# Edge weights scaled, and part of the window sums copied out of PSUM, by VectorE in place of ScalarE

## The chip, the cores and the metric

The kernel runs on one core of one Trainium2 chip. The metric is the device time of one launch in microseconds (us); lower is better. A core has several engines that run their own instruction streams in order and wait for one another through semaphores: TensorE (PE in the profile, with its weight loads as PEld), VectorE (DVE), ScalarE (ACT), GpSimd (POOL) and SyncE (SP). ScalarE, GpSimd and SyncE issue DMAs here. Matmuls write to PSUM, a small memory that GpSimd and the DMAs cannot use; everything else on the chip lies in SBUF.

## The reference

A graph layer on 12,500 nodes and 400,000 edges. For each edge, a small network turns 16 edge numbers into 192 weights; the source node's mapped row (160 numbers) is multiplied by them and by the edge's own four numbers, and the products are summed over the edges of each destination node. The edges come sorted by destination.

```python
h = maximum(layernorm(x), 0)                # per node
x0, x1 = h[:, :64], h[:, 64:].reshape(n, 32, 3)
y0 = x0 @ W_l1_0 * a / sqrt(64);  y1 = einsum('nuc,uv->nvc', x1, W_l1_1) * a / sqrt(32)
w = silu(edge16 @ fc_W1 / sqrt(16)) @ fc_W2 / sqrt(64)        # 192 weights per edge
w_a, w_b, w_c, w_d = w[:, :64], w[:, 64:128], w[:, 128:160], w[:, 160:]
e0, e1 = e4[:, :1], e4[:, 1:]               # e4: four numbers per edge
mid_a = w_a * y0[src] * e0
mid_d = w_d * einsum('euc,ec->eu', y1[src], e1) / sqrt(3)
mid_b = (w_b * y0[src])[:, :, None] * e1[:, None, :]
mid_c = (w_c * e0)[:, :, None] * y1[src]
z = sum over edges, by dst, of mid_a, mid_d (96 numbers) and mid_b, mid_c (96 x 3)
out = x + c_s * self_connection(h) + c_x * linear(z) * a
```

The scalar e0 multiplies only w_a and w_c. The kernel keeps the weights in the order a, c, b, d, so that these are the first 96 of the 192 columns.

## The kernel before, in words

**Nodes first.** A first stage normalizes the nodes, maps them, and writes the mapped rows to a table y_d in device memory. Its lines 324 to 384 (batch_norm, transposes, L373's copies out of PSUM, L384's addition) matter here only as rows from which durations can be read. L129 to L181 then prepare the edges' offsets.

**The edge loop.** The edges stand in 3125 tiles of 128. A batch b is four tiles (GT = 4), so there are 782 batches. Three tiles that follow each other share a window of 32 nodes (WT = 3, WN = 32), four windows make a group (GW = 4), so a group is 12 tiles or three batches, k = 0, 1, 2. A batch goes through these steps:

- `load(b)` (L456 to L476): GpSimd issues four indirect DMAs (gathers, L474), one for each tile, that fetch the source nodes' rows from y_d into a tile yg. There are 12 buffers of yg, and loads are issued ten batches ahead (AHEAD = 10). Ten batches, numbers 12, 24 and so on to 120, take their rows from a second table yr_d by one DMA of SP instead (L471). SP also loads the edge network's input, xe (L465).
- `hidden_pair` (L483, L488): every fourth batch, TensorE computes the hidden layer for two pairs of batches and ScalarE applies the activation (hT).
- `weigh(b)` (L505): four matmuls put the 192 weights of each edge into a PSUM tile pw, of which there are two. Then `scale` lets ScalarE multiply the first 96 columns of each tile by e0 in place (L421, four instructions of 128x96) and copy e1 and the edge's window offset behind the weights (L422, 16 numbers).
- `select(b)` (L536, L538): VectorE builds the selection matrix sel from pw's last columns: which of the 32 nodes an edge belongs to, alone and times each of e1's three numbers.
- `products(b)` (L427 to L434): VectorE multiplies yg with the weights in pw, into pr. L427 is the first instruction to read yg, so it waits for the gathers.
- `sums(b)` (L556): TensorE multiplies sel with pr for each tile and sums a window in a PSUM tile pz, of which there are two. When a window is complete, ScalarE copies it to the SBUF tile zs: 192 columns from the last 32 partitions (L561), and 64 columns from each of three other sets of 32 partitions (L563).
- `turn`, `linear`, `add` (L571 to L594), for the group before, in batches k = 0, 1, 2: TensorE transposes zs, ScalarE copies it out (za, L573), TensorE applies the output weights, ScalarE copies that out (os, L582, L583) while VectorE makes a placement matrix (place, L586), and TensorE places the rows among 256 nodes.
- `accumulate` (L599 to L603), in batch k = 2: VectorE loads the node tile's number into a register and adds the result to acc, two instructions.

TensorE, ScalarE and VectorE run these in the order in which the program writes them (a manual schedule); the semaphores are put in by the framework. GpSimd and SP run their loads in order, as buffers allow. The order of one batch is this:

```python
            for b in range(NB):
                ...
                if b + 2 < NB:
                    weigh(b + 2)
                if g:
                    (turn, linear, add)[k](g - 1)
                if b + 1 < NB:
                    select(b + 1)
                    products(b + 1)
                if g and k == K - 1:
                    accumulate(g - 1)
                    leave_before(g)
                sums(b)
                if b % 4 == 0 and b + 4 < NB:
                    hidden_pair((b + 4) // 2)
```

After the loop the last group is finished and the rest of acc is stored. A second path (L659 on), for edges too far from their window, is in the program, but these inputs do not enter its loop; it also calls `scale`.

Of the kernel before, what the change touches and what calls it, by code (L numbers as in the profile page):

```python
# [12 lines left out]
AF = mybir.ActivationFunctionType  # L13
# [5 lines left out]
P = 128  # L19
# [5 lines left out]
NW = 2 * M0 + 2 * M1  # L25
# [20 lines left out]
def kernel(  # L46
# [19 lines left out]
    nc = tc.nc  # L66
# [7 lines left out]
    NB = (T + GT - 1) // GT  # L74
# [342 lines left out]

    def scale(pw, ev, n):

        for k in range(n):  # L420
            nc.scalar.activation(pw[:, k, 0:96], pw[:, k, 0:96], AF.Copy, scale=ev[:, k, 0:1])  # L421
        nc.scalar.activation(pw[:, :n, NW:NW + 4], ev[:, :n, 1:5], AF.Copy)  # L422

    def multiply(pr, tmp, wt, yg, n):

        y1 = yg[:, :n, M0:].rearrange("p t (c u) -> p t c u", c=3)
        nc.vector.tensor_tensor(tmp[:, :n, 0:3, :], y1, wt[:, :n, NW:NW + 3].unsqueeze(3).to_broadcast([P, n, 3, M1]),  # L427
                                ALU.mult)
        nc.vector.tensor_reduce(tmp[:, :n, 3, :], tmp[:, :n, 0:3, :].rearrange("p t c u -> p t u c"), AX.X, ALU.add)  # L429
        nc.vector.tensor_mul(pr[:, :n, 192:PC], wt[:, :n, 96:160], yg[:, :n, 0:M0])  # L430
        nc.vector.tensor_mul(pr[:, :n, 0:M0], wt[:, :n, 0:M0], yg[:, :n, 0:M0])  # L431
        nc.vector.tensor_mul(pr[:, :n, 96:192].rearrange("p t (c u) -> p t c u", c=3),  # L432
                             wt[:, :n, M0:96].unsqueeze(2).to_broadcast([P, n, 3, M1]), y1)
        nc.vector.tensor_mul(pr[:, :n, M0:96], wt[:, :n, 160:NW], tmp[:, :n, 3, :])  # L434

    with (
# [11 lines left out]
        blocks, ev4, hids, rows, wts, sels, z_ps, z_sb, zT, o_sb, prs, sums_ps = ({} for _ in range(12))  # L448

        def tiles_of(b):  # L450
            return list(range(b * GT, min((b + 1) * GT, T)))
# [4 lines left out]
        def load(b):  # L456
            blk = b * GT // BT
            if blk not in blocks:

                xe = ld.tile([P, 512], F32, name="xe")  # L460
                v = e16[blk * P:(blk + 1) * P, :].rearrange("(s k f) (h c) -> s h f k c", s=4, k=2, h=2)
                for s in range(4):
                    for h in range(2):
                        lo = 32 * s + FC_IN * h
                        nc.sync.dma_start(xe[lo:lo + FC_IN, :].rearrange("p (k c) -> p k c", k=2), v[s, h])  # L465
                blocks[blk] = xe
            yg = ygp.tile([P, GT, D], F32, name="yg")
            rows[b] = yg
            r = made(b)
            if r is not None:  # L470
                nc.sync.dma_start(yg, by_tile(yr_d[r * GT * P:(r + 1) * GT * P, :]))  # L471
                return
            for k, t in enumerate(tiles_of(b)):
                nc.gpsimd.indirect_dma_start(  # L474
                    out=yg[:, k, :], out_offset=None, in_=y_d,
                    in_offset=bass.IndirectOffsetOnAxis(ap=src_sb[:, t:t + 1], axis=0))  # L476
# [14 lines left out]
        def hidden_pair(s):  # L491

            pair = [i for i in (s, s + 1) if 2 * i < NB]
            for i, ph in [(i, hidden(i)) for i in pair]:
                activate(i, ph)

        def weigh(b):
            hT = hids[b // 2]
            pw = p_w.tile([P, GT, 256], F32, name="pw")
            n = len(tiles_of(b))  # L500
            for k in (0, 2, 1, 3):
                if k < n:
                    r = slice(FC_H * (k // 2), FC_H * (k // 2 + 1))
                    o = P * (b % 2 * 2 + k % 2)
                    nc.tensor.matmul(pw[:, k, 0:NW], hT[r, o:o + P], w2[r, :], start=True, stop=True)  # L505
            scale(pw, e4_of(b), n)
            wts[b] = pw

        def e4_load(q):

            if q * EG < NG and q not in ev4:
                lo, hi = q * EG * TG, min((q + 1) * EG * TG, TP)
                raw = ld.tile([P, EG * TG, 4], F32, name="raw")
                nc.sync.dma_start(raw[:, :hi - lo, :].rearrange("p t c -> p (t c)"), e4[:, lo * 4:hi * 4])
                ev = evp.tile([P, EG * TG, 5], F32, name="ev")
                ev4[q] = ev, raw, lo, hi - lo

        def e4_join(q):
            if q in ev4:
                ev, raw, lo, n = ev4[q]  # L520
                nc.scalar.activation(ev[:, :n, 0:4], raw[:, :n, :], AF.Copy)
                nc.scalar.activation(ev[:, :n, 4:5], drel[:, lo:lo + n].unsqueeze(2), AF.Copy)

        def e4_of(b):
            g, k = divmod(b, TG // GT)
            o = g % EG * TG + k * GT
            return ev4[g // EG][0][:, o:o + GT, :]
# [13 lines left out]
        def products(b):  # L541
            wt, yg = wts.pop(b), rows.pop(b)
            pr = prod.tile([P, GT, PC], F32, name="pr")
            tmp = prod.tile([P, GT, 4, M1], F32, name="tmp")
            multiply(pr, tmp, wt, yg, len(tiles_of(b)))
            prs[b] = pr

        def sums(b):
            pr = prs.pop(b)
            for k, t in enumerate(tiles_of(b)):  # L550
                g, w = t // TG, t // WT % GW
                if t % WT == 0:
                    z_ps[g, w] = p_z.tile([P, 512], F32, name="pz")
                pz = z_ps[g, w]
                last = t % WT == WT - 1 or t == T - 1
                nc.tensor.matmul(pz[:, 0:PC], sels[g][:, t % TG, :, :], pr[:, k, :], start=t % WT == 0, stop=last)  # L556
                if last:
                    if w == 0:
                        z_sb[g] = post.tile([P, ZC], F32, name="zs")
                    pz, zs = z_ps.pop((g, w)), z_sb[g][WN * w:WN * (w + 1), :]  # L560
                    nc.scalar.activation(zs[:, 0:192], pz[96:P, 0:192], AF.Copy)  # L561
                    for c in range(3):
                        nc.scalar.activation(zs[:, 192 + M0 * c:192 + M0 * (c + 1)],  # L563
                                             pz[WN * c:WN * (c + 1), 192:PC], AF.Copy)
# [41 lines left out]
        def leave_before(g):  # L606

            for k, (lo, i) in enumerate(FLOORS):
                if lo == g:
                    store(FLOORS[k - 1][1] if k else 0, i)  # L610
# [5 lines left out]
        with order:  # L616
            for b in range(min(AHEAD, NB)):
                load(b)
            e4_load(0)
            e4_join(0)  # L620
            hidden_pair(0)
            weigh(0)
            if NB > 1:
                weigh(1)
            select(0)
            products(0)
            for b in range(NB):
                g, k = divmod(b, K)
                if b + AHEAD < NB:
                    load(b + AHEAD)  # L630
                q, r = divmod(b, EG * K)
                if r == 0:
                    e4_load(q + 1)
                if r == EG * K - 4:
                    e4_join(q + 1)
# [4 lines that stand above are left out]
                if b + 1 < NB:  # L640
                    select(b + 1)
                    products(b + 1)
                if g and k == K - 1:
                    accumulate(g - 1)
                    leave_before(g)
# [3 lines that stand above are left out]
            for h in ([NG - 2] if NG > 1 else []) + [NG - 1]:  # L649
                for k, stage in enumerate((turn, linear, add, accumulate)):  # L650
                    if h == NG - 1 or min(k, K - 1) > (NB - 1) % K:
                        stage(h)
                        if k == 3:
                            leave_before(h + 1)
# [4 lines left out]
    with (  # L659
# [10 lines left out]
        n = nc.values_load(far_i[0:1, 0:1], min_val=0, max_val=1)  # L670
        with tc.For_i(0, n, 1) as _:
            with tc.For_i(0, ZR, P) as r:
                nc.sync.dma_start(z_d[ds(r, P), :], zero)
            with tc.For_i(0, TP // GT, 1) as g:
# [4 lines left out]
                ev = fp.tile([P, GT, 5], F32, name="f_ev")  # L679
# [19 lines left out]
                pw = fpw.tile([P, GT, 256], F32, name="f_pw")  # L699
# [7 lines left out]
                for k in range(GT):  # L707
# [6 lines left out]
                    for c in range(3):  # L714
                        nc.scalar.activation(m[:, 192 + M0 * c:192 + M0 * (c + 1)], pr[:, k, 192:PC], AF.Copy,
                                             scale=ev[:, k, 1 + c:2 + c])
# [10 lines left out]
                    pz = fpp.tile([P, ZC], F32, name="f_pz")  # L727
                    nc.tensor.matmul(pz, sel, m, start=True, stop=True)
                    zs = fp.tile([P, ZC], F32, name="f_zs")
# [63 lines left out]
```

## Time and profile before

| what | value |
|---|---|
| median of three runs | 4068.4 us (4061.18 to 4073.2) |
| the profiled execution | 4061.72 us |
| its span | 4059.8 us |
| TensorE's mean granted clock | 0.933 |
| busy: PE, DVE, ACT, POOL | 3235.3, 2922.8, 2692.2, 3018.0 us |
| gathers (L474) | 3085, mean 948 ns |
| edge loop, first L427 to last | 208.0 to 4044.1 us |

The profile is of one execution on the chip. The span is what the profiler recorded; the execution's own time is 1.9 us longer. Times are in microseconds from the start of the span unless marked ns. A row of the costliest groups names line, engine, operation, the tiles (output<-inputs), the shapes (partitions x elements) and the count; then busy time and the mean of one in ns; then the engine's idle time just before these instructions and what ended most of it. "issue" means that the engine waited for nothing that the profile shows. In the waits, a line gives engine, instruction, what it waited for, the total, the number of times and the longest. DVEq is VectorE's sequencer, which handles waits and registers ahead of the engine itself.

### The profile page before, as it was taken

Reading aid. Unit: us, or ns where it says so; the run is one execution under the profiler, and the core shown is the slowest. Engines: PE = TensorE matmul, PEld = TensorE weight load, DVE = VectorE, ACT = ScalarE, POOL = GpSimd, SP = SyncE. Lnnn points to the kernel's source line nnn. Section 1 sums busy time; section 2 is a strip of 40 time slices with the busy share of each in tenths; the row PEclk is TensorE's granted clock in tenths of the full one; section 3 lists DMA queues with packets and bytes.
Section 4 is the critical chain, followed back from the end, with each engine's and each line's share of the span. In section 5 each row is a group of like instructions: output and inputs, shape, how many; then the busy total and the mean of one; then the engine's idle time right before and its main releaser. Section 6 shows DMA issues by size and latency. Waiting matters only on the chain.

```text
span 4059.8 us, 62554 instructions
## 1 busy us (share of the span) xinstructions
PE 3235.3 (80%) x17505; PEld 2347.5 (58%) x17505; DVE 2922.8 (72%) x7558; ACT 2692.2 (66%) x9543; POOL 3018.0 (74%) x3177
## 2 busy tenths in 40 slices
PE   6588888878787787887877887878777788778777
PEld 5466666555555555555555555555555555555555
DVE  7787777776777777777777777767777777777776
ACT  5477777766666666666666666666666666666665
POOL 7477777777777777777777777777777777777776
PEclk9899999999989989999999999999999989999998
DMA  6333333332322233323233332323232323243233
GB/s 192 88 84 83 80 83 80 76 76 74 77 74 74 74 76 74 77 74 76 72 76 75 75 76 74 74 74 77 74 76 74 76 72 76 75 124 75 72 81 78
DMA packets 244949, 326.49 MB, mean 80 GB/s; under 512 B 67290, under 2 KB 194342, under 8 KB 244342
## 3 DMA queue, kind: packets, MB, share of 16 engines
q0 software_dynamic: 151280, 256.22, 25.7%
q1 hardware_dynamic: 74322, 54.52, 4.7%
q10 hardware_dynamic: 18996, 11.72, 0.9%
q8 instruction: 141, 2.31, 0.2%
q14 instruction: 210, 1.72, 0.1%
HBM read 302.92 MB, written 19.28 MB: 79 GB/s over the span
## 4 chain that ended last, share of the span: by engine, by line
DVE 25%; POOL 23%; DMA 21%; issue 21%; PE 5%; ACT 1%; DVEq 1%; ACTq 0%; POOLq 0%
POOL yg L474 23%; DMA yg<-y_d,src_sb 21%; DVE tmp L429 5%; DVE tmp L427 5%; DVE pr L432 3%; DVE pr L431 2%; DVE acc L603 2%; DVE pr L434 2%; DVE sel L538 2%; PE pz L556 2%; DVE pr L430 2%; DVE sel L536 1%; PE pw L505 1%; PE px L483 1%; DVE place L586 1%
## 5 line engine op out<-in xcount | busy, mean ns | idle before, releaser
L474 POOL DMA_INDIRECT yg<-y_d,src_sb x3085 | 2925.3, 948 | 982.5 <-issue 745.8
L556 PE MATMUL pz<-pr,sel 128*128 128x256 f32 x6250 | 1623.9, 407 | 0.3 <-DVE pr L434 0.3
L421 ACT ACTIVATE pw<-pw,ev 128x96 f32<-128x96 f32 x3125 | 985.3, 315 | 858.3 <-PE pw L505 769.6
L556 PEld LDWEIGHTS pz<-pr,sel 128*128 128x128 f32 x6250 | 1237.4, 208 | 157.6 <-issue 0.9
L505 PE MATMUL pw<-w,hT 64*128 64x192 f32 x6250 | 758.5, 363 | 667.1 <-DVE pr L434 657.5
L427 DVE TENSOR_TENSOR tmp<-yg,pw 128x384 f32<-128x384 f32 x782 | 432.8, 553 | 972.3 <-DMA yg<-y_d,src_sb 970.8
L505 PEld LDWEIGHTS pw<-w,hT 64*128 64x128 f32 x6250 | 514.6, 194 | 1060.9 <-DVE pr L434 893.9
L563 ACT ACTIVATE zs<-pz 32x64 f32<-32x64 f32 x3126 | 669.9, 214 | 41.8
L429 DVE TENSOR_REDUCE tmp<-tmp 128x128 f32<-128x384 f32 x782 | 463.7, 593 | 27.0
L538 DVE TENSOR_TENSOR sel<-sel,pw 128x384 f32<-128x384 f32 x782 | 432.7, 553 | 27.0
L561 ACT ACTIVATE zs<-pz 32x192 f32<-32x192 f32 x1042 | 337.8, 324 | 148.3 <-PE pz L556 125.7
L432 DVE TENSOR_TENSOR pr<-pw,yg 128x384 f32<-128x384 f32 x782 | 428.8, 548 | 0.0
L483 PE MATMUL px<-xe,w 32*128 32x512 f32 x782 | 301.0, 656 | 81.8 <-issue 72.7
L488 ACT ACTIVATE hT<-px 128x512 f32<-128x512 f32 x391 | 218.5, 595 | 179.8 <-PE px L483 172.9
L431 DVE TENSOR_TENSOR pr<-pw,yg 128x256 f32<-128x256 f32 x782 | 324.1, 414 | 0.0
L430 DVE TENSOR_TENSOR pr<-pw,yg 128x256 f32<-128x256 f32 x782 | 323.8, 414 | 0.0
L536 DVE TENSOR_TENSOR sel<-iota,pw 128x128 f32<-128x128 f32 x782 | 218.8, 280 | 58.0 <-ACT pw L422 57.6
L580 PE MATMUL px<-wc,za 128*128 128x96 f32 (+1 forms) x1566 | 257.3, 305 | 0.4 <-ACT za L573 0.4
L580 PEld LDWEIGHTS px<-wc,za 128*128 128x128 f32 x1566 | 211.6, 205 | 62.2 <-issue 45.2
L434 DVE TENSOR_TENSOR pr<-pw,tmp 128x128 f32<-128x128 f32 x782 | 220.4, 282 | 0.0
L594 PE MATMUL px<-os,place 128*128 128x160 f32 x1044 | 219.0, 334 | 0.5 <-ACT os L583 0.5
L603 DVE SCALAR_TENSOR_TENSOR acc<-px,a_sb,acc 128x160 f32 x522 | 198.5, 380 | 12.2 <-PE px L594 2.7
(97 smaller groups left out, 1742.0 us busy)
## 6 DMA issues: line engine op xcount, KB each, us to landing
yg<-y_d,src_sb POOLq DMA_INDIRECT x3085
xe<-in_e SPq DMA_DIRECT2D x784, 32.0 KB
y_d<-ys ACTq DMA_DIRECT2D x12, 640.0 KB
acc<-in_x SPq DMA_DIRECT2D x11, 640.0 KB
out<-acc SPq DMA_DIRECT2D x11, 640.0 KB
raw<-in_e SPq DMA_DIRECT2D x32, 192.0 KB
yr_d<-ys ACTq DMA_DIRECT2D x5, 640.0 KB
yg<-yr_d SPq DMA_DIRECT2D x10, 320.0 KB
```

The costliest lines, as they stand in the source:

```text
L421: nc.scalar.activation(pw[:, k, 0:96], pw[:, k, 0:96], AF.Copy, scale=ev[:, k, 0:1])
L427: nc.vector.tensor_tensor(tmp[:, :n, 0:3, :], y1, wt[:, :n, NW:NW + 3].unsqueeze(3).to_broadcast([P, n, 3, M1]), ALU.mult)
L429: nc.vector.tensor_reduce(tmp[:, :n, 3, :], tmp[:, :n, 0:3, :].rearrange("p t c u -> p t u c"), AX.X, ALU.add)
L430: nc.vector.tensor_mul(pr[:, :n, 192:PC], wt[:, :n, 96:160], yg[:, :n, 0:M0])
L431: nc.vector.tensor_mul(pr[:, :n, 0:M0], wt[:, :n, 0:M0], yg[:, :n, 0:M0])
L432: nc.vector.tensor_mul(pr[:, :n, 96:192].rearrange("p t (c u) -> p t c u", c=3), wt[:, :n, M0:96].unsqueeze(2).to_broadcast([P, n, 3, M1]) ...
L474: nc.gpsimd.indirect_dma_start(out=yg[:, k, :], out_offset=None, in_=y_d, in_offset=bass.IndirectOffsetOnAxis(ap=src_sb[:, t:t + 1], axis=0))
L505: nc.tensor.matmul(pw[:, k, 0:NW], hT[r, o:o + P], w2[r, :], start=True, stop=True)
L538: nc.vector.tensor_tensor(sel[:, :, 0:3, :], sel[:, :, 3:4, :].to_broadcast([P, n, 3, WN]), wt[:, :n, NW:NW + 3].unsqueeze(3).to_broadcast ...
L556: nc.tensor.matmul(pz[:, 0:PC], sels[g][:, t % TG, :, :], pr[:, k, :], start=t % WT == 0, stop=last)
L563: nc.scalar.activation(zs[:, 192 + M0 * c:192 + M0 * (c + 1)], pz[WN * c:WN * (c + 1), 192:PC], AF.Copy)
L580: nc.tensor.matmul(po[:m, lo:hi], za[:, k, :m], wc[:, k, lo:hi], start=k == 0, stop=k == 1)
```

## The change

VectorE does three things that ScalarE did. `scale` becomes two VectorE instructions on a whole batch: a copy of e4's columns, and one multiplication of 128 x 4 x 96 elements in place in PSUM, with e0 stretched over 96 columns. The call of `scale` is taken out of `weigh` and put into a new function `apply`, which stands after `products(b + 1)` for batch b + 2, so on VectorE the scaling of a batch comes one batch ahead of its use. And the first 192 columns of each window are copied out of PSUM by VectorE. The three copies of 64 columns, the activations, za and os stay on ScalarE. In the built program, ScalarE's three copies of a window wait for VectorE's copy of the same window. The number of gathers, matmuls and DMAs is the same.

```diff
     def scale(pw, ev, n):
 
-        for k in range(n):
-            nc.scalar.activation(pw[:, k, 0:96], pw[:, k, 0:96], AF.Copy, scale=ev[:, k, 0:1])
-        nc.scalar.activation(pw[:, :n, NW:NW + 4], ev[:, :n, 1:5], AF.Copy)
+        nc.vector.tensor_copy(pw[:, :n, NW:NW + 4], ev[:, :n, 1:5])
+        nc.vector.tensor_mul(pw[:, :n, 0:96], pw[:, :n, 0:96], ev[:, :n, 0:1].to_broadcast([P, n, 96]))
...
-            scale(pw, e4_of(b), n)
             wts[b] = pw
+
+        def apply(b):
+
+            scale(wts[b], e4_of(b), len(tiles_of(b)))
...
-                    nc.scalar.activation(zs[:, 0:192], pz[96:P, 0:192], AF.Copy)
+                    nc.vector.tensor_copy(zs[:, 0:192], pz[96:P, 0:192])
...
             weigh(0)
+            apply(0)
             if NB > 1:
                 weigh(1)
             select(0)
             products(0)
+            if NB > 1:
+                apply(1)
             for b in range(NB):
...
                 if b + 1 < NB:
                     select(b + 1)
                     products(b + 1)
+                if b + 2 < NB:
+                    apply(b + 2)
                 if g and k == K - 1:
                     accumulate(g - 1)
                     leave_before(g)
```

## The prediction

> **What bounds the kernel now.** I read the page's shares of the span first, then its costliest groups, then two long windows of the edge loop, then the waits, then the order of time.
>
> ```profile
> PE 3235.3 (80%) x17505; PEld 2347.5 (58%) x17505; DVE 2922.8 (72%) x7558; ACT 2692.2 (66%) x9543; POOL 3018.0 (74%) x3177
> ...
> L474 POOL DMA_INDIRECT yg<-y_d,src_sb x3085 | 2925.3, 948 | 982.5 <-issue 745.8
> ...
> L421 ACT ACTIVATE pw<-pw,ev 128x96 f32<-128x96 f32 x3125 | 985.3, 315 | 858.3 <-PE pw L505 769.6
> ...
> L427 DVE TENSOR_TENSOR tmp<-yg,pw 128x384 f32<-128x384 f32 x782 | 432.8, 553 | 972.3 <-DMA yg<-y_d,src_sb 970.8
> ...
> L432 DVE TENSOR_TENSOR pr<-pw,yg 128x384 f32<-128x384 f32 x782 | 428.8, 548 | 0.0
> ```
>
> No engine is full by these shares. The two windows tell more (columns: length, then busy time and count of PE, PEld, DVE, ACT, POOL):
>
> ```profile
> 1000.00:2000.00 1000.00, 802.29 (x4268) 578.40 (x4267) 707.25 (x1800) 661.28 (x2381) 756.29 (x801) 0.93 0.30 75
> 2000.00:3000.00 1000.00, 796.75 (x4267) 574.58 (x4266) 707.48 (x1801) 661.79 (x2383) 756.30 (x800) 0.94 0.30 75
> ```
>
> GpSimd issues 1601 gathers in 2000 us: one every 1.25 us, 0.95 busy and 0.30 of issue, without a break. A batch has four, so 5.0 us, and a group of three batches 15.0 us. What VectorE waits for says the same:
>
> ```profile
> DVE tmp L427 <- DMA yg<-y_d,src_sb: 970.8, 687, 5.9
> PEld pw L505 <- DVE pr L434: 893.9, 520, 5.5
> ...
> DVE sel L536 <- ACT pw L422: 57.6, 52, 16.3
> ```
>
> So GpSimd's gathers set the end, VectorE waits for them in 687 of 782 batches, and TensorE waits for VectorE. ScalarE, which the change relieves, is waited for in 57.6 us only, 16.3 of it once at the start of the loop. One VectorE batch in order of time:
>
> ```profile
> 2005.90 0.56 DVE L427 TENSOR_TENSOR tmp<-yg,pw 128x384 f32<-128x384 f32 x1 [1.90 <-DMA yg<-y_d,src_sb]
> ...
> 2007.00 0.41 DVE L430 TENSOR_TENSOR pr<-pw,yg 128x256 f32<-128x256 f32 x1
> 2007.33 0.41 DVE L431 TENSOR_TENSOR pr<-pw,yg 128x256 f32<-128x256 f32 x1
> ...
> 2008.89 0.55 DVE L538 TENSOR_TENSOR sel<-sel,pw 128x384 f32<-128x384 f32 x1
> 2009.93 0.56 DVE L427 TENSOR_TENSOR tmp<-yg,pw 128x384 f32<-128x384 f32 x1 [0.48 <-DMA yg<-y_d,src_sb]
> ```
>
> The wait in brackets is VectorE's slack. Note also that L431 begins 0.33 after L430, which lasts 0.41: neighbours overlap by 0.08.
>
> **VectorE's need per group today.** From the first L427 (208.0) to the last (4044.1) are 3836 us and 781 batches. Less 971 of waiting for gathers and 41 for ScalarE, 2824 us remain: 3.62 a batch, 10.85 a group. Where L427 needs no wait it overlaps L538 by the 0.08 seen above, so a VectorE that never waits needs 10.6. The slack is 4.2 to 4.4 us in each 15.0. The question is whether the added work fits.
>
> **Part by part.** Removed from ScalarE: 3125 scalings, 782 copies of e4's columns and 1042 copies of 192 columns: 985 + 146 + 338 us of its busy time. No one waits for these, so this gains nothing but the 41 us that VectorE waited, which the gathers hide.
>
> Added to VectorE per group: three copies of e4's columns (16 elements), three multiplications of 128x384 in PSUM, four copies of 32x192 out of PSUM. The rows nearest:
>
> ```profile
> L339 DVE TENSOR_TENSOR ra<-ra,a_sb 128x8 f32<-128x8 f32 x12 | 2.0, 168 | 0.4
> L142 DVE CAST tile_i<-first 128x261 int32<-128x261 f32 x1 | 0.3, 298 | 0.0
> L161 DVE TENSOR_SCALAR at<-off,node_of 32x261 f32<-32x261 f32 x4 | 1.8, 443 | 0.1
> L599 DVEq TENSOR_LOAD <-tile_i x261: 298/304/929, 231.1 to 4047.6; - x131
> ```
>
> - Columns: 8 elements took 0.168; I take 0.165, and 0.035 more because the multiplication waits for it (L427, 0.56, is followed by the dependent L429 after 0.59). 3 x 0.20 = 0.60. Ends: 0.14 (L157, one element) and 0.28 (L536, 128 elements).
> - Multiplication: L432 has its size, a PSUM input and a stretched operand: 0.55. No VectorE row writes PSUM. Low end 0.47 (overlap as above); high end 0.95, if reading and writing one PSUM tile took turns, 384 more steps of 1.04 ns (L430 to L432: 0.135 for 128). On ScalarE writing PSUM is no dearer: L421's 315 for 96 elements lies under the 345 that L373's rows (398 for 160, 531 for 320, into SBUF) give for 96. I take 0.55.
> - Copies out: between L434 (128 elements, 0.282) and L430 (256, 0.414) lies 0.35 for 192. Ends: 0.26 (L142's rate) and 0.443 (L161).
> - Overlap lost: these copies start on other partitions than their neighbours. L161 does too, and its four take 1.81, that is 0.45 each at 0.443: no overlap. So a copy costs 0.36 and the multiplication before it its full 0.565; the accumulation before it loses 0.10.
> - Accumulation (L603): the sequencer now passes the multiplication's wait before it loads the tile's number: 0.30 for the load and two register steps of 0.09, with gaps 0.6 after the multiplication begins. Today L430 to L434 cover that. One multiplication in three costs 0.62.
>
> Sum: 0.60 + 2 x 0.565 + 0.62 + 4 x 0.36 + 0.10 = 3.9 a group. VectorE then needs 10.6 + 3.9 = **14.5 of 15.0**. With all low ends the addition is 2.9, with all high ends 5.8: 13.5 and 16.4 (4493 us by the formula that follows).
>
> **Where that begins to cost.** If VectorE never waited, the span would be 209.5 (end of the first batch) + 260.3 groups + 14.7 (last product to the end, 4045.1 to 4059.8). It passes 4059.8 at 14.73 a group, and each 0.1 above costs 26 us. One stretch is tighter: ten of the batches 12 to 120 come from yr_d over SP, so GpSimd is through with batch 130 at 188 + 120 x 5.0 = 788. VectorE at 14.5 gets there at 209.5 + 130 x 4.83 = 838, 50 us late. The 12 buffers of yg let GpSimd run ahead 11 batches, 55 us, so nothing is lost; at 14.6 it stalls, 4 us for each further 0.1. The delay is worked off at 0.5 a group.
>
> **The added waits.** ScalarE's three copies of 64 columns now wait for VectorE's copy of the same window; queued behind them are hT, za and os. The turn of a group waits for both. Counted from the end of the products of a group's first batch: columns and multiplication 0.8, accumulation 0.8, two copies 0.7, then ScalarE's three at 0.22: about 3.1, while TensorE has its weigh matmuls done at 0.95. That idles TensorE 2.2 in a group. Its work there is 11.6 (three weighs 2.8, turn 0.55, linear 0.9, add 0.8, three sums of 1.89, three quarters of a hidden pair of 1.13), so 13.8 of 15.0: it fits. VectorE asks for a batch's sums only after the next batch's products, some 6 us later, when they are done. Pieces like L556 at 3.42 in place of 1.89 follow idle stretches of TensorE, so this cover is thin. The end of the kernel has the new steps in series: 1 to 2 us.
>
> **GpSimd itself.** It can be slowed: under VectorE's L384, with two inputs in SBUF, a gather took 1.97 in place of 0.95.
>
> ```profile
> 99.44 1.47 DVE L384 TENSOR_TENSOR acc<-acc,ys 128x1280 f32<-128x1280 f32 x1
> ...
> 99.76 1.97 POOL L304 DMA_INDIRECT xr<-in_x,src_sb  x1 [0.30 <-issue]
> ```
>
> The loop's operations with one input in PSUM leave it at 0.94 to 0.95, and the new ones all have one side in PSUM, so I take no loss. Were each of the 1042 copies out to put off a gather by its own 0.35, it would be 365 us; nothing in the loop's rows points there.
>
> The Trainium skill, "Perfetto Trace Analysis", section Optimizing Scalar/DVE Operations, speaks against the change: a VectorE instruction pays about 60 ns for access in SBUF and about 125 ns in PSUM. L430 (PSUM input) begins its successor 0.33 later, 0.065 over its 256 steps, and L384 (SBUF only) has 0.065 over its 1280, so this trace shows no difference; by the page the ten new instructions would cost some 0.6 a group more, an estimate that would make the time about 4150. The skill's "SBUF — State Buffer", section Who interferes with whom, says that VectorE copies hold a port pair against GpSimd; L384 shows such a hold, and the page confines it to two SBUF inputs or the fast SBUF-to-SBUF modes, which these are not; by the page the sum stays as it is.
>
> **Rivals.**
> 1. VectorE becomes the bound: each small surplus counts ten times a group. Place: VectorE's own queue. It decides from 14.73 on; at 15.0 the span is 224.2 + 260.3 x 15.0 = 4129, at 14.9 4103. For it: the sum is within 0.25 of the limit. Against: every term is from a row of the same shape. 25%.
> 2. The multiplication in place runs at 0.95: 14.5 + 1.2 = 15.7, 4311. For it: no row shows VectorE writing PSUM. Against: ScalarE's rows. 6%.
> 3. TensorE's idle time at the turn, with slow pieces after it, holds up VectorE's copies: 0.3 a group more is 14.8, 4077 to 4085. 5%.
> 4. Faster, by a chain through ScalarE that I overlooked: at most the 41 us that VectorE waited for it, of which the gathers leave little; 4045. 4%. That the change does not do what it says I exclude: in the built program's order of instructions the ScalarE entries are gone and VectorE's are there.
>
> **The numbers.** Likeliest, 60%: the gathers still set the end, 4061.7 (the profiled execution: span 4059.8 and 1.9 around it) becomes about 4064. That execution is 6.7 under the median 4068.4 of the three runs, so in terms of the median 4070, with its own range 4057 to 4080. About 0.3%, 12 us, is what a measurement tells from no change: same 60%, slower 25 + 6 + 5 = 36%, faster 4%. The range reaches to rival 1 at 15.0 (4129 + 8) and leaves out rival 2: 4057 to 4140.
>
> **What would show it.** Right: POOL's gathers 1.25 us apart from batch 130 on; L427's wait falls from 971 us to under 150 and lies in the second half; VectorE's busy share is 90% or more; the multiplication lasts 0.55, the copy 0.35. Wrong: gathers with gaps over 0.30 that end with VectorE's products throughout (rival 1 or 2, told apart by the multiplication's mean); VectorE's copies waiting for TensorE (rival 3); gathers over 0.95 (GpSimd's port).

## The result and the profile after

The changed kernel takes 4220.4 us (median of four runs, 4206.8 to 4230.0); the kernel before, on the same chip, 4067.8 us (four runs, 4061.2 to 4073.2). The ratio is 1.037, with a 95% interval of 1.034 to 1.040: slower by some 153 us, where 4070 was forecast. The profiled execution of the changed kernel took 4226.5 us, with a span of 4224.6.

From here on lines carry the numbers of the changed kernel: L420 copies e4's columns, L421 is the multiplication, L426 to L433 are the products, L538 and L540 select, L473 the gathers, L504 weigh, L558 the sums, L563 VectorE's copy of a window and L565 ScalarE's three, L573 the turn, L575 za, L582 linear, L596 add, L605 the accumulation, L482 and L487 the hidden pair and hT.

The page's shares of the span, the granted clock in 40 slices, and five of the costliest groups:

```profile
PE 3490.5 (83%) x17505; PEld 2439.5 (58%) x17505; DVE 3841.9 (91%) x10164; ACT 1250.8 (30%) x4594; POOL 3025.3 (72%) x3177
...
PEclk9799998888999889898989899988889889988898
...
L473 POOL DMA_INDIRECT yg<-y_d,src_sb x3085 | 2932.5, 951 | 1081.0 <-issue 770.0
...
L565 ACT ACTIVATE zs<-pz 32x64 f32<-32x64 f32 x3126 | 669.9, 214 | 2443.1 <-DVE zs L563 2405.3
...
L563 DVE COPY zs<-pz 32x192 f32<-32x192 f32 x1042 | 376.2, 361 | 184.1 <-PE pz L558 154.2
...
L421 DVE TENSOR_TENSOR pw<-pw,ev 128x384 f32<-128x384 f32 x782 | 442.4, 566 | 26.7
...
L426 DVE TENSOR_TENSOR tmp<-yg,pw 128x384 f32<-128x384 f32 x782 | 426.9, 546 | 0.0
```

VectorE is busy in 91% of the span, ScalarE in 30% instead of 66%. The operations cost what was forecast: the multiplication 0.566 us, the copy out 0.361. Two things are new. TensorE's busy time has grown by 255 us (3235 to 3490) for the same 17505 matmuls: the clock records add up to 921 us at half clock, 546 before. And ScalarE's copies of a window wait 2405 us for VectorE's copy. The longest waits of VectorE and of TensorE in the loop, and GpSimd's for products:

```profile
DVE zs L563 <- PE pz L558: 154.2, 119, 2.7
DVE pw L420 <- PE pw L504: 21.9, 15, 15.8
```

```profile
PE px L573 <- DVE zs L563: 231.8, 195, 2.7
PE pw L504 <- DVE pr L433: 167.8, 268, 1.4
PE px L482 <- issue: 100.8, 64, 2.4
PE px L596 <- ACT hT L487: 61.1, 64, 1.5
```

```profile
POOL yg L473 <- DVE pr L433: 131.9, 116, 5.4
```

L426 no longer waits for the gathers at all (its idle time is 0.0), and the gathers now wait for VectorE's products: 971 us of slack are gone, so VectorE sets the end. But it still waits, 154 us, for TensorE's sums, and nothing is left to hide that. Here is how such a wait comes about, in order of time, TensorE first, then two of its weight loads, then three VectorE rows:

```profile
1985.79 0.92 PE L504 MATMUL pw<-w,hT 64*128 64x192 f32 x8 [1.01 <-DVE pr L433]
1988.12 1.48 PE L573 MATMUL px<-ident,zs 128*128 128x128 f32 x3 [1.40 <-DVE zs L563]
1989.39 3.62 PE L558 MATMUL pz<-pr,sel 128*128 128x256 f32 x8
1992.94 2.08 PE L482 MATMUL px<-xe,w 32*128 32x512 f32 x4
1994.95 1.65 PE L504 MATMUL pw<-w,hT 64*128 64x192 f32 x8
```

```profile
1988.65 0.18 PEld L573 LDWEIGHTS px<-ident,zs 128*128 128x128 f32 x1 [0.35 <-ACT zs L565]
...
1989.12 0.18 PEld L573 LDWEIGHTS px<-ident,zs 128*128 128x128 f32 x1 [0.28 <-ACT zs L565]
```

```profile
1992.26 0.36 DVE L563 COPY zs<-pz 32x192 f32<-32x192 f32 x1 [0.19 <-PE pz L558]
...
1996.65 0.18 DVE L420 COPY pw<-ev 128x16 f32<-128x16 f32 x1 [0.45 <-PE pw L504]
...
1999.92 0.36 DVE L563 COPY zs<-pz 32x192 f32<-32x192 f32 x1 [2.50 <-PE pz L558]
```

TensorE idles 1.40 before the turn, and its three transposes take 1.48 (0.55 in the kernel before, median): the weight loads of the second and the third wait for ScalarE's copies, and the clock is halved already. The clock record puts TensorE at half clock from 1987.9 to 2001.6; the sums take 3.62 where 1.89 is usual, a hidden pair 2.08 for 1.13, weigh 1.65 for 0.92. VectorE comes to two window copies (L563) and to the column copy of its next batch (L420) before TensorE is done, and waits 0.19, 2.50 and 0.45 us.

Counting by groups of three batches, from L426 to L426: 66 of 260 groups have no half clock in them, and their period is 14.72 us (median). That is VectorE's own work. The mean of all is 15.35, and 224.2 + 260.3 x 15.35 = 4220 is the span within 5 us. The 0.63 on top is VectorE's waiting: of 155 us of waits of its copies, 153 have at least 1.5 us of half clock in the 4 us ahead of them, where half clock covers 22% of the span as a whole (921 of 4225).

### The profile page after: what moved, and what is told of

The parts are those of the page before. It is cut to its first block, busy times and chain, and to the rows that moved or that the text cites. A ratio compares the mean times of both kernels' runs of the same rounds, so it can differ in the third digit from the quotient of the medians.

```text
span 4224.6 us, 59393 instructions
## 1 busy us (share of the span) xinstructions
PE 3490.5 (83%) x17505; PEld 2439.5 (58%) x17505; DVE 3841.9 (91%) x10164; ACT 1250.8 (30%) x4594; POOL 3025.3 (72%) x3177
## 4 chain that ended last, share of the span: by engine, by line
DVE 42%; PE 16%; POOL 14%; issue 13%; DMA 10%; DVEq 1%; ACT 1%; ACTq 0%; POOLq 0%
POOL yg L473 14%; DMA yg<-y_d,src_sb 10%; PE pz L558 7%; DVE tmp L428 6%; DVE tmp L426 6%; DVE pr L431 5%; DVE zs L563 4%; DVE pr L430 4%; DVE pr L429 3%; DVE acc L605 3%; DVE pw L421 3%; PE px L482 3%; PE pw L504 3%; DVE sel L538 2%; DVE pr L433 2%
## 5 line engine op out<-in xcount | busy, mean ns | idle before, releaser
L473 POOL DMA_INDIRECT yg<-y_d,src_sb x3085 | 2932.5, 951 | 1081.0 <-issue 770.0
L558 PE MATMUL pz<-pr,sel 128*128 128x256 f32 x6250 | 1734.8, 428 | 0.0
L558 PEld LDWEIGHTS pz<-pr,sel 128*128 128x128 f32 x6250 | 1308.2, 220 | 186.3 <-issue 0.9
L565 ACT ACTIVATE zs<-pz 32x64 f32<-32x64 f32 x3126 | 669.9, 214 | 2443.1 <-DVE zs L563 2405.3
L504 PE MATMUL pw<-w,hT 64*128 64x192 f32 x6250 | 776.9, 370 | 182.8 <-DVE pr L433 167.8
L504 PEld LDWEIGHTS pw<-w,hT 64*128 64x128 f32 x6250 | 531.7, 200 | 609.9 <-DVE pr L433 311.0
L563 DVE COPY zs<-pz 32x192 f32<-32x192 f32 x1042 | 376.2, 361 | 184.1 <-PE pz L558 154.2
L573 PE MATMUL px<-ident,zs 128*128 128x128 f32 (+1 forms) x783 | 261.0, 367 | 294.0 <-DVE zs L563 231.8
L421 DVE TENSOR_TENSOR pw<-pw,ev 128x384 f32<-128x384 f32 x782 | 442.4, 566 | 26.7
L540 DVE TENSOR_TENSOR sel<-sel,pw 128x384 f32<-128x384 f32 x782 | 432.5, 553 | 27.0
L482 PE MATMUL px<-xe,w 32*128 32x512 f32 x782 | 341.4, 740 | 106.9 <-issue 100.8
L426 DVE TENSOR_TENSOR tmp<-yg,pw 128x384 f32<-128x384 f32 x782 | 426.9, 546 | 0.0
L573 PEld LDWEIGHTS px<-ident,zs 128*128 128x128 f32 (+1 forms) x783 | 116.5, 160 | 455.2 <-DVE zs L563 202.4
L596 PE MATMUL px<-os,place 128*128 128x160 f32 x1044 | 212.8, 326 | 63.2 <-ACT hT L487 61.1
L582 PE MATMUL px<-wc,za 128*128 128x96 f32 (+1 forms) x1566 | 250.5, 299 | 16.2 <-ACT hT L487 15.7
L582 PEld LDWEIGHTS px<-wc,za 128*128 128x128 f32 x1566 | 206.5, 201 | 80.4 <-issue 39.8
L538 DVE TENSOR_TENSOR sel<-iota,pw 128x128 f32<-128x128 f32 x782 | 224.4, 287 | 24.6
L605 DVE SCALAR_TENSOR_TENSOR acc<-px,a_sb,acc 128x160 f32 x522 | 200.3, 384 | 31.3 <-issue 3.8
```

Of the source, the lines that this page charges most:

```text
L421: nc.vector.tensor_mul(pw[:, :n, 0:96], pw[:, :n, 0:96], ev[:, :n, 0:1].to_broadcast([P, n, 96]))
L473: nc.gpsimd.indirect_dma_start(out=yg[:, k, :], out_offset=None, in_=y_d, in_offset=bass.IndirectOffsetOnAxis(ap=src_sb[:, t:t + 1], axis=0))
L482: nc.tensor.matmul(ph, w1[r, :], xe[r, :], start=True, stop=True)
L563: nc.vector.tensor_copy(zs[:, 0:192], pz[96:P, 0:192])
L582: nc.tensor.matmul(po[:m, lo:hi], za[:, k, :m], wc[:, k, lo:hi], start=k == 0, stop=k == 1)
```

## The experiments

Three theories were stated first. **Theory 1**: VectorE's own 14.7 us a group, and on top TensorE's idle time before the turn, half clock after it, and VectorE's copies waiting for that. **Theory 2**: VectorE's own work alone. **Theory 3**: ScalarE's new wait for VectorE's copy delays what is queued behind it (hT, za, os), and these delay TensorE. Theory 4 was added after e13: own work and waits add up, 26 us for each 0.1 a group, because VectorE's slack is used up. Theory 2 falls by the trace already: 14.72 alone gives 224.2 + 260.3 x 14.72 = 4056.

The runs fell on chips of two kinds. On the first kind (the result above, and e13 to e17; e13 ran on one chip and e14 to e17 on another) the kernel before takes 4062 to 4068 us. On the second (e1 to e12, e18) the same kernel takes 5758 to 5889 us: the instructions of VectorE, ScalarE and GpSimd last as long, but the engines stop together. In the changed kernel there (e9) TensorE, VectorE and ScalarE stand idle at once 247 times for over 1 us after 250 us from the start, 716 us in all (median 2.7, longest 13.8); in the changed kernel on the first kind never. Only ratios to the kernel before on the same chip can be compared there.

### e1 to e12, on chips of the second kind

The edits. Late turn (e1, e5, e10), and the same lines in the kernel before (e11):

```diff
-                if g:
-                    (turn, linear, add)[k](g - 1)
+                if k and g:
+                    (turn, linear)[k - 1](g - 1)
+                if k == 0 and g > 1:
+                    add(g - 2)
...
-                if g and k == K - 1:
-                    accumulate(g - 1)
-                    leave_before(g)
+                if k == 0 and g > 1:
+                    accumulate(g - 2)
+                    leave_before(g - 1)
...
```

ScalarE's copies first (e2): in `sums`, the line of VectorE's copy stands behind the loop of ScalarE's three in place of ahead of it.

```diff
-                    nc.vector.tensor_copy(zs[:, 0:192], pz[96:P, 0:192])
                     for c in range(3):
                         nc.scalar.activation(zs[:, 192 + M0 * c:192 + M0 * (c + 1)],
                                              pz[WN * c:WN * (c + 1), 192:PC], AF.Copy)
+                    nc.vector.tensor_copy(zs[:, 0:192], pz[96:P, 0:192])
```

The window copy alone (e3: the kernel before with only its L561 on VectorE), and the multiplication alone (e4, e6, e12: the changed kernel with that copy back):

```diff
-                    nc.vector.tensor_copy(zs[:, 0:192], pz[96:P, 0:192])
+                    nc.scalar.activation(zs[:, 0:192], pz[96:P, 0:192], AF.Copy)
```

Repeated weigh ahead of the turn (e7), and the accumulation behind the copies (e8: `sums(b)` ahead of `accumulate`):

```diff
-        def weigh(b):
+        def weigh(b, times=1):
...
-            for k in (0, 2, 1, 3):
+            for k in (0, 2, 1, 3) * times:
...
-                    weigh(b + 2)
+                    weigh(b + 2, 2 if g and k == 0 else 1)
```

> The changed kernel with turn, linear and add (and accumulate) of a group issued one batch later, so that TensorE no longer stands before the turn until VectorE's last window copy. VectorE's and ScalarE's work is the same. Theory T1 (VectorE's own work is 14.7 us a group, as in the shortest groups of the changed kernel, and the rest of its mean of 15.4 comes from TensorE: it idles before the turn, runs at half clock afterwards, and VectorE's copies then wait for it): 4060 to 4090 us, TensorE's granted clock back at 0.92 or more, VectorE's wait for pz under 40 us. Theory T2 (VectorE's work alone passes what the gathers leave): unchanged, 4200 to 4230 us.

> The changed kernel with ScalarE's three copies of a window ahead of VectorE's, so that ScalarE no longer waits for VectorE and the turn waits for VectorE's copy alone. The turn's wait shrinks by about 0.7 to 0.9 us a group. T1: a part of the loss goes, 4100 to 4180 us. T2: unchanged, 4200 to 4230 us. A third theory, T3 (ScalarE's new wait of 2405 us delays hT and os, and these delay TensorE): most of the loss goes, 4060 to 4100 us.

> The kernel before with one part of the change alone: the 192 columns copied by VectorE, the scaling on ScalarE as before. VectorE then needs 10.85 + 1.6 = 12.4 of 15.0 us a group; the turn still waits for VectorE's copy. T1 and T2: the gathers set the end, 4060 to 4080 us, T1 with a granted clock under 0.93. T3: 4080 to 4150 us, since the wait of ScalarE is the same as in the changed kernel.

> The changed kernel with the 192 columns copied by ScalarE again: the scaling and e4's columns on VectorE alone. VectorE needs 14.7 - 1.6 = 13.1 of 15.0 us a group, and nothing waits for its copies. T1, T2 and T3: the gathers set the end, 4060 to 4080 us. If it is over 4100 us, writing PSUM from VectorE has a price that the rows of single instructions do not show.

> The turn, linear and add of a group stand one batch later in TensorE's order, so that the four windows have been copied when TensorE comes to the turn; all operations are the same. On a chip where the kernel before takes about 4068 us and the changed one 4220: by theory 1 (TensorE idles before the turn, works at half clock afterwards, and VectorE's copies wait for it) 4080 to 4130, with VectorE's waits for the sums (154 us in the changed kernel) and for the weigh matmuls (22 us) down by more than half. By theory 2 (VectorE's own work alone) 4200 to 4230. By theory 3 (ScalarE's wait for VectorE's copies delays hT and os) 4190 or more, since that wait stays.

> Only the scaling and e4's columns go to VectorE; the 192-column copy is ScalarE's again. VectorE's work per group is 14.7 less four copies of 0.36 = 13.3 us, under the gathers' 15.0, and nothing on TensorE waits for VectorE's queue at the turn. Theory 1 and theory 2: 4062 to 4085, with GpSimd's gathers 1.25 us apart again. If the multiplication in PSUM itself were the loss: 4180 or more.

> The changed kernel with the weigh matmuls in front of the turn issued twice (same values into the same place): TensorE works through 0.9 us of the time in which it idled in each group. If the loss comes by way of the half clock that follows the idle time (theory 1, its second half): 4130 to 4190 and less half-clock time than the changed kernel's 921 us. If idle time alone delays VectorE: 4215 to 4235. Theory 2: 4220, unchanged.

> The changed kernel with the accumulation behind the copies of the windows in VectorE's queue: the two copies that the turn waits for come 0.8 us earlier, VectorE does the same work, except that a copy may now wait for sums that the accumulation covered. Theory 1: 4160 to 4205, with TensorE's wait before the turn (434 us for VectorE's copies) nearly halved. Theory 2: 4215 to 4225.

> The changed kernel itself, beside the others of this call on one chip. Where the kernel before takes about 4068 us: 4205 to 4230. On chips like those of the runs so far (before at 5760 to 5890 us, where all compute engines stop for about 8 us at a time): theory 1 expects a ratio to before of 0.99 to 1.01, above that of the late turn (0.951 and 0.964) and of the multiplication alone (0.961 and 0.975) by two per cent or more, since the wait at the turn costs there too; theory 2 expects it level with the late turn.

> The changed kernel with turn, linear and add one batch later. Where before takes about 4068 us: theory 1 4080 to 4130, theory 2 4200 to 4230. On the other kind of chip: theory 1 2 to 5% under the changed kernel, theory 2 within 0.5% of it.

> The kernel before with turn, linear and add one batch later: the control for the late turn. Where before takes about 4068 us, the gathers set the end: 4062 to 4075. On the other kind of chip: if the late turn only takes away a wait that the change brought in (theory 1), 0.99 to 1.005 of before; if it helps any kernel there, 0.97 or less, and its gain in the changed kernel says nothing about the change.

> The scaling and e4's columns on VectorE, the 192-column copy on ScalarE. Where before takes about 4068 us: 4062 to 4085 by theories 1 and 2, 4180 or more if the multiplication in PSUM is the loss. On the other kind of chip: 0.96 to 0.98 of before, as measured, and under the changed kernel.

Measured, in us; e1 to e4, e5 to e8 and e9 to e12 ran on one chip each:

| run | time | before there | ratio (95%) |
|---|---|---|---|
| e1 late turn | 5596.6 | 5888.7 | 0.951 (0.945 to 0.957) |
| e2 ScalarE's copies first | 5884.1 | 5888.7 | 1.000 (0.995 to 1.005) |
| e3 window copy alone | 5786.3 | 5888.7 | 0.982 (0.976 to 0.987) |
| e4 multiplication alone | 5658.7 | 5888.7 | 0.961 (0.956 to 0.966) |
| e5 late turn | 5548.2 | 5759.0 | 0.964 (0.961 to 0.968) |
| e6 multiplication alone | 5615.0 | 5759.0 | 0.975 (0.971 to 0.979) |
| e7 repeated weigh | 5718.0 | 5759.0 | 0.993 (0.990 to 0.997) |
| e8 accumulation behind | 5718.5 | 5759.0 | 0.993 (0.991 to 0.996) |
| e9 the changed kernel | 5629.8 | 5758.2 | 0.976 (0.969 to 0.982) |
| e10 late turn | 5548.2 | 5758.2 | 0.963 (0.957 to 0.968) |
| e11 before, late turn | 5644.7 | 5758.2 | 0.977 (0.970 to 0.984) |
| e12 multiplication alone | 5617.4 | 5758.2 | 0.973 (0.967 to 0.979) |

Here the change makes the kernel faster by 2.4%. The waits of the changed kernel on such a chip (e9) tell what is different:

```profile
PE px L573 <- DVE zs L563: 597.4, 149, 9.5
PEld px L573 <- issue: 494.6, 187, 9.8
...
DVE pw L420 <- remote: 455.4, 85, 17.6
...
PE px L482 <- remote: 303.2, 52, 8.0
```

At L482, in the middle of the hidden pair, TensorE stops 52 times for 5.8 us each (303 / 52), "remote" meaning that nothing recorded released it; in the changed kernel on the first kind of chip the same line has 64 stops of 1.6 us, called "issue" (100.8 / 64, above). These stops recur at the same matmuls, 256 apart, on both kinds of chip: 61 of the 64 places of the changed kernel on the first kind are stops in e9 too. The DMA part of the page shows 142 loads of 16 KB of code on one instruction queue and 185 of 8 KB on the other here (210 in the kernel before), so loads of code are the likely cause; no run took them away, and it stays a guess. The control e11 failed its purpose: the late turn helps the kernel before as well, by 2.3%. So theory 1 gets nothing from the late turn's gain on these chips, and e2, level with the kernel before and 2.4% above what e9 shows for the changed kernel, spoke against theory 3 here. As the first kind shows, these chips answer another question: with stops like these, who bounds the loop is different, and their ratios don't carry over.

### e13, late turn on the first kind of chip

> The changed kernel with turn, linear and add one batch later. Where the kernel before takes about 4068 us and the changed one 4220: theory 1 (TensorE idles before the turn, works at half clock afterwards, and VectorE's copies wait for it) 4080 to 4130 with half-clock time near the 546 us of the kernel before; theory 2 (VectorE's own work alone) 4200 to 4230; theory 3 (ScalarE's wait) 4190 or more. Where before takes 5760 to 5890 us: 0.951 to 0.964 of it again.

Measured: 4201.7 us against 4062.6 before, ratio 1.034 (1.033 to 1.037). Of the changed kernel's 153 us over the kernel before, 139 are left. The waits of TensorE, and VectorE's first row:

```profile
PE pw L504 <- DVE pr L433: 381.2, 430, 1.6
PE px L596 <- ACT hT L487: 116.1, 61, 2.1
PE px L482 <- issue: 101.1, 64, 1.9
PE px L582 <- ACT hT L487: 95.8, 65, 1.5
```

```profile
DVE zs L563 <- PE pz L558: 98.8, 115, 1.8
```

The wait before the turn is gone from the list and half clock is down from 921 to 656 us, as theory 1 wanted, but the time stayed. **Theory 1 as put has fallen.** Its second half stands: all of the 99 us that VectorE's copies still wait has half clock right ahead of it (at least 1.5 us in the 4 us before). What is left points to ScalarE: TensorE waits 212 us for hT (61 + 16 in the changed kernel), whose activation stands in ScalarE's queue behind the copies that wait for VectorE. The late turn also lengthens VectorE's own group from 14.72 to 14.83 (median of the groups without half clock), by the place matrix behind the copy.

### e14, multiplication alone

> Only the scaling and e4's columns on VectorE, the 192-column copy on ScalarE. Where before takes about 4065 us, theory 4 (VectorE's own work of 14.7 us a group has used up its slack, and its waits for TensorE, 160 us in the changed kernel, come on top): own work 13.25 a group, no copy that waits for TensorE, the gathers set the end: 4058 to 4080. If the multiplication in PSUM is the loss in itself: 4180 or more.

Measured: 4064.1 against 4062.6, ratio 1.000 (0.999 to 1.001). VectorE waits for the gathers again:

```profile
DVE tmp L426 <- DMA yg<-y_d,src_sb: 410.4, 465, 5.9
```

So the multiplication in place in PSUM and e4's columns cost nothing in the end, though they take 560 of the 971 us of slack. The loss needs the third part, the window copy; whether that part alone brings a loss on the first kind of chip, no run shows (e3 ran on the second).

### e15, half the multiplication

```diff
-        nc.vector.tensor_mul(pw[:, :n, 0:96], pw[:, :n, 0:96], ev[:, :n, 0:1].to_broadcast([P, n, 96]))
+        nc.vector.tensor_mul(pw[:, :n, 0:48], pw[:, :n, 0:48], ev[:, :n, 0:1].to_broadcast([P, n, 48]))
```

> The changed kernel with the scaling of columns 0 to 47 alone, columns 48 to 95 left unscaled: VectorE's own work is 192 steps of about 1.04 ns shorter in each batch, 0.6 us a group, and every wait of the changed kernel is still there. Where before takes about 4065 us: theory 4: 14.1 of its own and 0.65 of waiting are 14.75, some groups behind the gathers: 4070 to 4110. Theory 1 as first put (the wait at the turn with half clock sets the pace by itself): 4180 or more.

Measured: 4108.4 against 4062.6, ratio 1.012 (1.010 to 1.013). All waits of the changed kernel are still there, VectorE's among them:

```profile
DVE zs L563 <- PE pz L558: 147.9, 130, 2.8
```

VectorE waits 148 us, nearly as before, and of the 153 us over the kernel before 46 are left, because its own work is 0.4 a group less (14.33 in place of 14.72; 0.6 was expected, but the accumulation's register load now shows, 46 us of issue before L605). Own work and waits add up, as theory 4 has it: 14.33 and 148 / 260 = 0.57 make 14.90, and the mean period is 14.91. By the formula that is 224.2 + 260.3 x 14.91 = 4105, the span 4106.4.

### e16, ScalarE's copies first

> The changed kernel with ScalarE's three copies of a window ahead of VectorE's copy, so that ScalarE no longer waits for it (2405 us in the changed kernel) and hT, za and os are not queued behind that wait. Where before takes about 4065 us: theory 3 (that wait delays hT, TensorE idles for it and runs at half clock after, VectorE waits): 4140 to 4190. If it does not matter, or VectorE now waits for ScalarE's copies: 4210 to 4260.

Measured: 4096.4 against 4062.6, ratio 1.008 (1.007 to 1.010): 34 us over the kernel before in place of 153, by the order of two lines, with the same instructions. Better than theory 3's own forecast. VectorE's two longest rows of waiting (in this kernel L564 is ScalarE's three copies and L566 VectorE's), and the turn in order of time:

```profile
DVE zs L566 <- ACT zs L564: 24.4, 49, 3.1
DVE pw L420 <- PE pw L504: 15.9, 1, 15.9
```

```profile
2007.22 0.92 PE L504 MATMUL pw<-w,hT 64*128 64x192 f32 x8 [1.02 <-DVE pr L433]
2009.55 0.55 PE L573 MATMUL px<-ident,zs 128*128 128x128 f32 x3 [1.41 <-DVE zs L566]
2009.93 1.89 PE L558 MATMUL pz<-pr,sel 128*128 128x256 f32 x8
```

TensorE idles 1.41 before the turn, as it did in the changed kernel (1.40), so that wait by itself isn't the loss. But now ScalarE's six copies are done when VectorE's last copy ends, and the transposes run in 0.55 in place of 1.48. In the changed kernel ScalarE starts them only after VectorE's copies, one behind the other, 0.22 each, and TensorE waits for them between the transposes. The median length of the turn, from its first transposition to the end of its last, is 1.33 us in the changed kernel and 0.55 here. That 0.8 us is what a group's first window lacks. Take the stretch from the products of a group's first batch to VectorE's copy of its first window. With no half clock in it, the sums end 1.35 us before the copy in the changed kernel (79 of 258 groups) and 2.14 here (148 of 258; medians). A piece of sums at half clock needs some 1.7 us more (3.62 for 1.89). It fits into the second margin and not into the first. The traces bear that out: where these sums ran for over 1 us at half clock, VectorE's copy waited for them in 105 of 150 groups of the changed kernel and in none of 109 here; in the groups without half clock, in none of either. Half clock fell with it, from 921 to 461 us. **Theory 3 is right in its cause**, ScalarE's wait behind VectorE's copy, and the turn is one place where it acts.

### e17, both

> Late turn (4202 us where before takes 4063) and ScalarE's copies first, together: TensorE waits neither for VectorE before the turn nor for ScalarE's delayed hT (381 us on VectorE's products and 212 us on hT in the late turn are its waits). Theory 3 with theory 4: VectorE's own 14.83 a group and waits of 0.1 to 0.2 left: 224 + 260.3 x 14.93 to 15.03 = 4110 to 4140. If the remaining waits come from TensorE's own stops at new code: 4180 to 4205.

Measured: 4139.0, ratio 1.018 (1.017 to 1.020). VectorE waits 23 us for ScalarE's copies, but its group is longer: 14.99 (median without half clock). In this order the window copy ahead of the place matrix takes 0.39 to the next start where it took 0.29 in the changed kernel, and the place matrix 0.38 to 0.55 where it took 0.36. So the time lies in the range forecast, but not by its terms: 14.83 of own work and 0.1 to 0.2 of waits were expected. With VectorE as the bound, 0.1 us of its order counts as much as a wait: 26 us.

### e18, repeated weigh

> The changed kernel with the weigh matmuls ahead of the turn issued twice (same values into the same place), so that TensorE works through 0.9 us of the wait before the turn; VectorE's and ScalarE's work, order and waits stay. Where before takes about 4063 us and the changed kernel 4220: if the link between ScalarE's late copies and VectorE's waits is TensorE's half clock after idle time, half-clock time falls from 921 us to 700 or less and the time to 4110 to 4170. If the late release of hT and the late turn by themselves make VectorE wait, the clock may rise but the time stays at 4200 to 4235. Where before takes 5760 us: 0.993 of it, as measured.

It ran on the second kind of chip: 5809.2 against 5869.0, ratio 0.990 (0.988 to 0.993). So what less half clock alone would gain on the first kind, no run shows. That half clock is the link between ScalarE's late copies and VectorE's waits rests on the trace of the changed kernel: for the first window's sums VectorE waits in none of the 79 groups without half clock on the way and in 110 of the 179 with it, and 153 of 155 us of waits stand right behind half clock.

No version that ran on the first kind of chip (e13 to e17) beat the kernel before: with the gathers as the bound, e14 equals it.

## Why the prediction was wrong

- **What bounds the kernel before**: right. GpSimd's gathers, 15.0 us a group; e14 shows them again as soon as VectorE has slack.
- **The prices of the added operations**: right. Multiplication 0.55 taken, 0.566 measured; copy 0.35, 0.361; columns 0.165, 0.166. Rival 2 (0.95 in place) didn't come, nor did GpSimd slow down (951 ns a gather, 948 before).
- **VectorE's sum, 14.5**: short by 0.2; 14.72 is measured. The base of 10.6 was right; the steps from start to start were too small: 0.393 for a copy (0.36 taken), 0.597 for a multiplication ahead of a copy (0.565), and the place matrix behind a copy takes 0.36 to the next start where it took 0.26. By the formula 14.72 alone gives 224.2 + 260.3 x 14.72 = 4056: still no loss. But it left no slack.
- **"The added waits": this is the step that failed.** It named ScalarE's wait, and that hT, za and os are queued behind it, but it priced only the 2.2 us of idle time before the turn, and against TensorE's whole group: "13.8 of 15.0: it fits". A busy sum doesn't tell when a piece ends. VectorE does ask for a batch's sums "some 6 us later" (6.4 from the end of the products, in the changed kernel's groups without half clock), but for a group's first window that is nearly used up: the turn ends 3.7 us after the products and the sums 5.0, so 1.35 are left. A slow piece of sums, which the prediction names, takes 1.7, more than that, and stands at nothing in its sum. The measured price is 0.63 us a group, 164 us over 260 groups. e16 shows that 119 of the 153 us of loss come from the order of ScalarE's and VectorE's copies, e15 that the waits cost because VectorE is full.
- **Rival 3** was the right mechanism in its end (slow pieces after the turn hold up VectorE's copies), at 5% and 0.3 us a group, half its size. Its place, the idle time at the turn, was only partly right: e13 removed that and kept the loss.
- **Rival 1**: VectorE is the bound, as rival 1 has it, but by its own work it would be at 14.72, under the 14.73 from which it decides. The sum of rivals 1 and 3, each mild, was not considered as one case: a bound at the edge, and a wait that comes on top. That is why the range ended at 4140.
- The observations named in advance told the cases apart: L427's wait (now L426) went to nothing, gathers waited for products (132 us), and VectorE's copies waited for TensorE.
- The Trainium skill's "Perfetto Trace Analysis", Optimizing Scalar/DVE Operations, by the estimate worked out from it would have made the time about 4150, with some 60 ns more for each PSUM access. That is nearer to the result, but not for its reason: the steps of the copies and the multiplications from start to start exceed those forecast by some 0.03 us, and VectorE's whole sum by 0.2 a group, not 0.6. That e14 costs nothing doesn't decide it, since its slack would hide such a price.

## What to carry to other kernels

When work moves to an engine, add up its sum and its waits together: an engine filled to 98% of the bound pays for every wait that slack used to hide, however short. Price a new wait by what is queued behind it on the waiting engine, and by the margin between the moment a piece is ready and the moment it is asked for, not by busy shares. Where two engines write parts of one tile, the order in which the program writes the two can decide who waits for whom, as here: try both.

## What the runs showed of the hardware

- The same kernel took 4062 us on some chips and 5758 to 5889 on others, and the change was 3.7% slower on one kind and 2.4% faster on the other. Instructions of VectorE and GpSimd are as long on both (the multiplication 0.566 us on both, a gather 0.951 and 0.949); the difference is in the stops.
- TensorE's half clock comes in stretches of 3.4 us and multiples (109 of 166 are 3.4 us long in the changed kernel). The kernel before has 119 stretches, hidden by slack. The stretches of a run begin on a fixed grid of steps of 3.413 us, to within 4 ns in each of seven runs (before, after, e13 to e17). In the changed kernel's steps at full clock TensorE idled 1.55 us (median) where a step at half clock followed and 0.32 where none did; with over 1.7 us of idle time half clock followed in 64 of 64 steps, in e16 in 76 of 82.
- So it counts how idle time falls on this grid. In the changed kernel's turn shown above, the 1.01 us before the weigh matmuls and most of the 1.40 before the turn lie in one step (1984.48 to 1987.90, 2.19 us idle), and half clock begins at its end, ahead of the transposes: their waits can't have brought on that stretch. In e16's turn the 1.02 and the 1.41 lie in two steps, and full speed followed.
- VectorE and ScalarE copying different parts of one PSUM tile into different parts of one SBUF tile ran one after the other in the order of the program (2405 us of waiting in one order, 24 in the other). The semaphores that order them are the framework's, so no run shows whether the two engines could copy at once.
